# Two attention blocks on one core: a second Strassen step in layer 1's q, and the statistics of x on ScalarE

## The chip, the core and the metric

The kernel runs on one core of one Trainium2 chip. The metric is device time in microseconds, the median over three runs. The engines of the core work from queues of their own: TensorE (PE, with its weight loads shown apart as PEld), VectorE (DVE), ScalarE (ACT), GpSimd (POOL), and SyncE (SP), which issues most transfers. All data are float32. On PE a float32 matmul is two instructions in the profile, each with a weight load.

## What is computed

Two layers over eight samples of 512 channels x 1024 positions. Layer 0 is attention with eight heads after a norm over 32 groups. Layer 1, where the change lies, norms the whole sample with one mean and one variance, and has one head:

```python
def _L1_conv_ref(x, gn_gamma, gn_beta, wq, bq, wk, bk, wv, bv, wo, bo):
    mean = jnp.mean(x, axis=(1, 2, 3), keepdims=True)
    var = jnp.var(x, axis=(1, 2, 3), keepdims=True)
    n = (x - mean) * jax.lax.rsqrt(var + EPS)
    n = n * gn_gamma[None, :, None, None] + gn_beta[None, :, None, None]
    nf = n.reshape(b, c, h * w)
    q = jnp.einsum('oc,bcs->bos', wq, nf) + bq[None, :, None]
    k = jnp.einsum('oc,bcs->bos', wk, nf) + bk[None, :, None]
    v = jnp.einsum('oc,bcs->bos', wv, nf) + bv[None, :, None]
    attn = jnp.einsum('bci,bcj->bij', q, k) * c ** (-0.5)
    attn = jax.nn.softmax(attn, axis=-1)
    out = jnp.einsum('bcj,bij->bci', v, attn)
    out = jnp.einsum('oc,bcs->bos', wo, out) + bo[None, :, None]
    return x + out.reshape(b, c, h, w)
```

## The kernel before

**Folded weights.** Before the first sample the kernel multiplies layer 1's wq with wk (`wqk1`, L1728) and wv with wo (`wvo1`, L1725), so that layer 1 has one product "q" (x by wqk1, scored against x itself) and one product "v". Mean and deviation of x are taken out of the products: x goes into the matmuls as it is, and `Norm.untaken` (L350) and `Norm.bias` (L359) give small vectors that put the norm back.

**Strassen.** A product of 512 x 512 by 512 x 1024 is cut into 2 x 2 blocks and done with seven block products and not eight. The blocks are named A11 to A22 for the weights, B11 to B22 for the data; S1 to S4 are sums of A blocks, T1 to T4 differences of B blocks (`Combined.make`, L394, makes T1 to T4 of x on DVE, 128x1024 each). `strassen` (L414) runs the seven products for one row of blocks, c, in two banks of PSUM: `line` takes A11 B11, S2 T2, S3 T3 and A22 T4 one after the other in one running sum, whose values between are copied out (`copied`, ACT) or read (`done`); `single` takes A12 B21, S1 T1 and S4 B22. A product is written into a bank only when the bank's last value has been read. `together` (L607) takes turns between two such runs, c=0 and c=1, a step each.

**The second step.** Four of the seven products are plain (A12 B21, S1 T1, S4 B22, A22 T4); each can itself be cut into quarters and done with seven smaller ones. The kernel does so in layer 0's q and k and in layer 1's v: `by_two_steps` (L545) runs two pairs of such products in turns, then the three line products. It needs quarters of the data (`quarters_b`, L504: three DVE instructions, one of 128x512 and two of 128x256, for each of B21, T1, B22 and T4) and quarters of the weights (`WeightTwice`, L514: made once by DVE before the first sample, 16 sums of 128x128, stored to HBM by SP, and loaded for each use through ACT's queue, two transfers of 512 KB).

**A sample's order.** Layer 0's v, q and k, the scores and values of four head pairs, the projection (`project`, L1211, two `strassen` runs) whose `done` adds bias and the input to give x; then `attention1` (L1260): q (`make_q`, L1288, two `strassen` runs of one step), v (`make_v_twice`), scores, exponentials, values, output. The order on PE, ACT and DVE is written out by hand: each engine works in the order in which the code emits. `at_steps` (L619) runs a generator and after step n calls the functions that stand under n in a table of hooks; so DVE's other work is put between the products by number of step.

**Statistics of x.** In the projection `Norm.of_half` (L317) takes DVE's bn_stats of each 128x512 half chunk as soon as it is written, and after the stage `of_channels` (L320) aggregates four chunks. In q, `mean_of_all` (L325, after step 2) sends the chunk means through a small matmul on PE (`sample_average`, L296), reduces it on DVE and forms the spread with three DVE instructions; `deviation` (L335, after step 4) sends that through PE again, and POOL raises it to -1/2; `untaken` follows at step 5. `make_q`'s results leave by ACT with a scale per output row, the layer's gamma (L1296).

**Buffers.** PSUM has two tags, `s` and `o`, two buffers each of two banks; a `strassen` run takes one of each. SBUF tiles of 4 KB a partition come from one pool of 36 (`tile2`); weights from a pool of three (`wpool`).

## Time and profile before

| | us |
|---|---|
| median of three runs | 2830.75 (2830.41 to 2830.96) |
| the profiled execution | 2830.62 |
| its span, first to last instruction | 2828.9 |
| DVE 128x512 add out of PSUM (L1292), mean of one | 0.68 |
| DVE 128x512 bn_stats (L318), mean of one | 0.69 |
| DVE 128x1024 difference for T (L400), mean of one | 1.22 |
| ACT 128x512 copy out of PSUM (L425), mean of one | 0.58 |
| POOL 128x512 add (L1345), mean of one | 1.27 |
| POOL 128x256 add (L477), mean of one | 0.74 |
| POOL power of 128x1 (L339), mean of one | 1.46 |

The time of one is from its start to its end; on DVE and ACT the next instruction can begin some 0.1 before the end of the last. A stage is found by its lines: in the third sample the projection (L632 with `w_p`) goes from 938.70 to 963.33, layer 1's q (L632 with `w_wqk`) from 963.33 to 987.81, and v (L890) begins there.

### The profile page before, as it was taken

The page shows a single profiled execution, that of the slowest core. Times are in us where ns is not written, and L with a number is a line of the kernel's source. Part 1 is how long each engine was busy: PE and PEld are TensorE (multiplying, and loading weights), DVE is VectorE, ACT ScalarE, POOL GpSimd, SP SyncE. Part 2 cuts the span into 40 slices and gives each one's busy share as a digit, 9 for nine tenths or more (in the row PEclk, how much of TensorE's full clock was granted, in tenths as well). Part 3 has the DMA queues.
Part 4 walks back from the last instruction along what each step waited for, and adds up shares of the span by engine and source line. Part 5 has one row for each costly group of instructions (what it writes and reads, how often), then busy time and mean ns, then how long its engine had stood idle before and what let it go on. Part 6 is the DMA issues. An engine that isn't in the chain of part 4 may idle for free.

```text
span 2828.9 us, 38606 instructions
## 1 busy us (share of the span) xinstructions
PE 2815.1 (100%) x15496; PEld 1551.3 (55%) x15496; DVE 2124.3 (75%) x2979; ACT 1101.5 (39%) x1536; POOL 273.8 (10%) x236
## 2 busy tenths in 40 slices
PE   9999999999999999999999999999999999999999
PEld 5434765357643476445773456734567346673365
DVE  6677696767867778776777777777777776867867
ACT  3462324623256232552325523265232642326432
POOL 0000220003100040000400004000040000400011
PEclk9999999999999999999999999999999999999999
DMA  8422131321323213133131231313212141121001
GB/s 293 162 74 88 57 123 64 87 90 53 112 68 91 86 69 105 54 91 109 56 108 50 84 108 57 108 50 98 93 64 101 50 124 67 64 100 43 8 16 39
DMA packets 81123, 237.75 MB, mean 84 GB/s; under 512 B 21512, under 2 KB 22312, under 8 KB 74536
## 3 DMA queue, kind: packets, MB, share of 16 engines
q1 hardware_dynamic: 74456, 212.11, 23.2%
q10 hardware_dynamic: 6480, 23.10, 2.4%
q8 instruction: 124, 2.03, 0.3%
q14 instruction: 63, 0.52, 0.1%
HBM read 179.37 MB, written 31.98 MB: 75 GB/s over the span
## 4 chain that ended last, share of the span: by engine, by line
PE 92%; DVE 7%; issue 1%; ACT 0%; SPq 0%; DMA 0%; POOL 0%; DVEq 0%; ACTq 0%; POOLq 0%
PE s L941 15%; PE ps_o L960 15%; PE ps_q L632 8%; PE ps_v L647 7%; PE ps_o L1540 7%; PE ps_p L632 6%; PE ps_l_qk L869 5%; PE ps_l L1376 4%; PE ps_s L1359 4%; PE ps_s_qk L862 4%; PE ps_l_v L647 3%; PE ps_s L1376 3%; PE ps_o_qk L862 3%; PE ps_s_v L890 2%; PE ps_s_two L1670 2%; PE ps_o_v L890 1%
## 5 line engine op out<-in xcount | busy, mean ns | idle before, releaser
L798 ACT ACTIVATE p<-s 128x1024 f32<-128x1024 f32 x512 | 523.8, 1025 | 329.1 <-PE s L941 322.2
L800 DVE TENSOR_TENSOR acc<-acc,p 128x1024 f32<-128x1024 f32 x384 | 469.5, 1223 | 100.9 <-ACT p L798 92.9
L960 PE MATMUL ps_o<-p,v 64*64 64x512 f32 x4096 | 528.7, 589 | 0.0
L941 PE MATMUL s<-c_q,c_k 64*64 64x512 f32 x3584 | 465.1, 590 | 0.0
L960 PEld LDWEIGHTS ps_o<-p,v 64*64 64x64 f32 x4096 | 156.6, 133 | 282.8 <-issue 278.3
L941 PEld LDWEIGHTS s<-c_q,c_k 64*64 64x64 f32 x3584 | 134.7, 133 | 253.2 <-issue 236.1
L339 POOL TENSOR_TENSOR rstd<-rstd,minus_half 128x4 f32<-128x4 f32 (+1 forms) x16 | 19.8, 1241 | 2076.6 <-DVE rstd L338 2076.6
L1540 PE MATMUL ps_o<-t_p,s_v 128*128 128x512 f32 x384 | 168.2, 594 | 0.0
L800 DVE TENSOR_TENSOR acc<-p,p 128x1024 f32<-128x1024 f32 x64 | 78.3, 1223 | 80.0 <-ACT p L798 80.0
L1350 ACT ACTIVATE p<-p,factor 128x512 f32<-128x512 f32 (+1 forms) x112 | 85.3, 780 | 115.7 <-DVE p L1386 90.9
L1364 ACT COPY p<-ps_s 128x512 f32<-128x512 f32 x96 | 53.1, 588 | 178.7 <-PE ps_s L1359 178.7
L1540 PEld LDWEIGHTS ps_o<-t_p,s_v 128*128 128x128 f32 x384 | 72.3, 190 | 91.3 <-issue 89.2
L1386 DVE TENSOR_TENSOR p<-ps_l,p 128x512 f32<-128x512 f32 x136 | 90.1, 683 | 40.5 <-PE ps_l L1376 40.1
L632 PE MATMUL ps_q<-t,w_wqk 128*128 128x512 f32 x256 | 116.1, 598 | 0.0
L632 PE MATMUL ps_p<-t_p,w_p 128*128 128x512 f32 x256 | 112.6, 592 | 0.8 <-DVE inv L812 0.8
L425 ACT COPY u_v<-ps_v 128x512 f32<-128x512 f32 x48 | 28.1, 586 | 204.9 <-PE ps_v L647 179.6
L1386 DVE TENSOR_TENSOR p<-ps_s,p 128x512 f32<-128x512 f32 x112 | 74.8, 685 | 37.9 <-PE ps_s L1376 37.9
L647 PE MATMUL ps_v<-w_v,t_again 128*128 128x256 f32 x448 | 99.0, 379 | 0.0
L425 ACT COPY u_p<-ps_p 128x512 f32<-128x512 f32 x48 | 28.1, 586 | 169.3 <-PE ps_p L632 169.3
L425 ACT COPY u_q<-ps_q 128x512 f32<-128x512 f32 x54 | 31.3, 579 | 160.6 <-PE ps_q L632 160.6
L647 PEld LDWEIGHTS ps_v<-w_v,t_again 128*128 128x128 f32 x448 | 85.1, 190 | 11.6
L632 PE MATMUL ps_p<-o,w_p 128*128 128x512 f32 x192 | 88.6, 597 | 2.3 <-DVE o L980 2.3
(463 smaller groups left out, 4911.3 us busy)
## 6 DMA issues: line engine op xcount, KB each, us to landing
x<-in_x SPq DMA_DIRECT2D x92, 512.0 KB, 6.5
w_qk<-stored_qk SPq DMA_DIRECT2D x14, 1792.0 KB, 7.3
w_wqk<-stored_wqk SPq DMA_DIRECT2D x8, 1792.0 KB, 7.5
fold<-acc SPq DMA_DIRECT2D x56, 256.0 KB, 3.1
inv<-inv_rows SPq DMA_DIRECT2D x56, 256.0 KB, 5.0
qk_twice<-stored_qk_twice ACTq DMA_DIRECT2D x28, 512.0 KB, 6.6
w_wvo<-stored_wvo SPq DMA_DIRECT2D x8, 1792.0 KB, 7.5
out<-x SPq DMA_DIRECT2D x28, 512.0 KB, 4.6
```

The lines of the kernel that those rows point to most:

```text
L632: nc.tensor.matmul(bank, w[a][:, k, c * P : (c + 1) * P], bs[b][:, k, :], start=fresh and k == 0, stop=k == 1, skip_group_check=True,)
L647: nc.tensor.matmul(bank[:, u * 2 * P : (u + 1) * 2 * P], bs[b][:, k, n * P : (n + 1) * P], w[a][:, k, :], start=fresh and u == k == 0, sto ...
L798: nc.scalar.activation(p, s, AF.Exp, scale=factor)
L800: nc.vector.tensor_tensor(acc, first, p, ALU.add)
L862: nc.tensor.matmul(bank[:, i * 2 * P : (i + 1) * 2 * P], parts[a][x], twice_b[v][y], start=start and i == 0, stop=True, skip_group_check=True,
L869: nc.tensor.matmul(bank, of(i, a)[:, k, :], bs[v][:, k, :], start=start and k == 0, stop=k == 1, skip_group_check=True,)
L941: nc.tensor.matmul(s[cols, j, :], ks[pair][k0 // HALF][rows, k0 % HALF : k0 % HALF + HD], qs[pair][g][rows, :], start=True, stop=True,)
L960: nc.tensor.matmul(o[cols, half, :], vs[kt][rows, c0 : c0 + HD], p[rows, j, :], start=kt == 0, stop=kt == NT - 1,)
L1359: nc.tensor.matmul(bank, bs[v][:, k, t * P : (t + 1) * P], q_parts[a][:, k, :], start=a == "A11" and k == 0, stop=k == 1, skip_group_check ...
L1376: nc.tensor.matmul(bank[:, u * 2 * P : (u + 1) * 2 * P], v[y][:, u * P : (u + 1) * P], a[x], start=start and u == 0, stop=True, skip_group ...
L1386: nc.vector.tensor_tensor(at(r, t), bank, at(r, t), ALU.add)
L1540: nc.tensor.matmul(bank, v_parts[kt // 2][a][:, kt % 2, c * P : (c + 1) * P], p_parts[kt // 2][b][:, kt % 2, cols], start=fresh and kt == ...
```

## The change

q of layer 1 gets the second step. `make_q` becomes one generator of 20 steps with its own order: of the pair A12 B21 with S4 B22 two products, both line products A11 B11, the other five products, both S2 T2, the seven products of the pair S1 T1 with A22 T4, both S3 T3. One pair runs at a time, in two banks of tag `s`; the two lines take one `o` buffer each. The projection's hooks load the weights' quarters (`ready.load`) and make the quarters of B22 and B21; T1's and T4's are made in q.

The statistics of x leave DVE: `moments` has ACT go over a half chunk twice, once for the mean and once for the squares around the first half's mean, with the sums taken by the accumulator; six half chunks in the projection's `done`, the last two in q after steps 1 and 2. `both_halves` joins them with seven POOL instructions of 128x4, and the three of the spread go to POOL too. `mean_of_all` moves to step 9, `deviation` to 10, `untaken` to 14.

The scale per output row can no longer be applied on the way out, so gamma is multiplied into both sides of wqk1 before the first sample: eight DVE instructions with a row of gamma (a new input, broadcast to all partitions by one DMA) take the place of eight ACT instructions, and `WeightTwice("wqk1")` is made and stored after that of qk02.

```diff
+        def scale_both(self, by, row):
+            for cc in range(NC):
+                for to, a in self.moving(cc):
+                    nc.vector.scalar_tensor_tensor(
+                        a, a, vec[:, by + cc : by + cc + 1], row[:, to], ALU.mult, ALU.mult
+                    )
...
+        def pass_over(self, cc, half, name, func, **args):
+            to = onepool.tile([P, HALF], FP, tag="held", name=f"{name}_{self.name}_{cc}_{half}")
+            nc.scalar.activation(to, piece(self.xs, cc, half), func, **args)
+
+        def moments(self, cc, half, first):
+            mean, part = self.stat[:, 0, cc : cc + 1], self.part[:, cc, 0 if first else 1, :]
+            self.pass_over(
+                cc, half, "mean", AF.Identity, scale=1.0 / HALF,
+                accum_out=mean if first else part[:, 1:2],
+            )
+            self.pass_over(
+                cc, half, "square", AF.Square, bias=mean, scale=-1.0, accum_out=part[:, 0:1]
+            )
+
+        def both_halves(self):
+            mean, var = self.stat[:, 0, :], self.stat[:, 1, :]
+            (q0, q1), d = (self.part[:, :, i, 0] for i in range(2)), self.part[:, :, 1, 1]
+            nc.gpsimd.tensor_tensor(d, d, mean, ALU.subtract)
+            nc.gpsimd.tensor_tensor(q0, q0, q1, ALU.add)
+            nc.gpsimd.tensor_scalar(d, d, 0.5, None, ALU.mult)
+            nc.gpsimd.tensor_scalar(var, q0, 1.0 / N, None, ALU.mult)
+            nc.gpsimd.tensor_tensor(mean, mean, d, ALU.add)
+            nc.gpsimd.tensor_tensor(d, d, d, ALU.mult)
+            nc.gpsimd.tensor_tensor(var, var, d, ALU.subtract)
...
         def mean_of_all(self):
+            engine = nc.gpsimd if self.width == 1 else nc.vector
...
+    PAIRS_Q = [[("A12", "B21"), ("S4", "B22")], [("S1", "T1"), ("A22", "T4")]]
...
@@ project: done @@
-                    norm.of_half(chunk, half)
+                    if i == half or i == 1:
+                        norm.moments(chunk, half, i == half)
+                    if (i, half, c) == (1, 0, 1):
+                        ready.halve("B21")
...
+        hooks[0] = [ready.load]
+        hooks[7] = [lambda: ready.halve("B22")]
+        at_steps(together(project(w, 0), project(w, 1)), hooks)
-        for cc in range(NC):
-            norm.of_channels(cc)
...
+    class Ready:
+        def __init__(self, xs, b):
+            self.combine, self.quarters, self.b = Combined(f"1_{b}"), {}, b
+            self.combine.take(xs)
+        def load(self):
+            self.weights = WeightTwice("wqk1")
+        def halve(self, name):
+            self.quarters[name] = quarters_b(
+                self.combine.parts[name], tile2(f"{name}_twice_{self.b}")
+            )
...
+        def make_q(w):
+            parts = ready.weights.all(columns_of(w))
+            first, second = ([tile2(f"{n}_q_1_{b}_{r}") for r in range(2)] for n in ["c11", "c22"])
+            lines = [banks("o", f"ps_l{r}_q_1_{b}")[:, 0, :] for r in range(2)]
+            def pair(products, to, name):
+                line, single = (banks("s", f"ps_{name}{n}_q_1_{b}")[:, 0, :] for n in range(2))
+                def add(at, bank):
+                    nc.vector.tensor_tensor(at, bank, at, ALU.add)
+                for bank, x, y, start, use, r, t in [
+                    (line, "A11", "B11", True, nc.scalar.copy, 0, 0),
+                    (single, "A12", "B21", True, add, 0, 0),
+                    (line, "S2", "T2", False, nc.scalar.copy, 0, 1),
+                    (single, "S1", "T1", True, nc.scalar.copy, 1, 1),
+                    (line, "S3", "T3", False, add, 1, 1),
+                    (single, "S4", "B22", False, add, 0, 1),
+                    (line, "A22", "T4", False, nc.scalar.copy, 1, 0),
+                ]:
+                    for i, (a, v) in enumerate(products):
+                        nc.tensor.matmul(
+                            bank[:, i * 2 * P : (i + 1) * 2 * P], parts[a][x], twice_b[v][y],
+                            start=start and i == 0, stop=True, skip_group_check=True,
+                        )
+                    use(
+                        to[r][:, :, t * 2 * P : (t + 1) * 2 * P],
+                        bank.rearrange("p (i q) -> p i q", i=2),
+                    )
+                    yield
+            def multiply(r, a, v, fresh):
+                by_channels(w.parts[0], r, bs)(lines[r], a, v, fresh)
+            def final(r, i, half, x, y):
+                n = r + 2 * i
+                nc.vector.scalar_tensor_tensor(
+                    piece(qs, n, half), x, norm.c[:, n : n + 1], y, ALU.add, ALU.add
+                )
+            def take(r):
+                c11 = first[r][:, 0, :]
+                nc.vector.tensor_tensor(c11, lines[r], c11, ALU.add)
+            def c12_of(r):
+                c12 = first[r][:, 1, :]
+                nc.vector.tensor_tensor(c12, lines[r], c12, ALU.add)
...
+            quarters = pair(PAIRS_Q[1], second, "s")
+            for n in range(7):
+                next(quarters)
+                if n == 2:
+                    c12_of(0)
+                if n == 4:
+                    c12_of(1)
+                yield
+            for r in range(2):
+                nc.scalar.activation(
+                    piece(qs, r, 0), first[r][:, 0, :], AF.Identity, bias=norm.c[:, r : r + 1]
+                )
+                final(r, 0, 1, second[r][:, 0, :], first[r][:, 1, :])
+            for r in range(2):
+                multiply(r, "S3", "T3", False)
+                for n, half in enumerate([1, 0]):
+                    final(r, 1, half, lines[r], second[r][:, n, :])
+                yield
+
+        at_steps(make_q(w), {
+            1: [lambda: norm.moments(0, 1, False), lambda: combine.make(1)],
+            2: [lambda: norm.moments(1, 1, False)],
+            3: [lambda: combine.make(2), norm.both_halves],
+            7: [lambda: combine.make(4)],
+            8: [lambda: twice_w.append(WeightTwice("wvo1"))],
+            9: [norm.mean_of_all, lambda: ready.halve("T1")],
+            10: [norm.deviation, lambda: ready.halve("T4")],
+            12: [lambda: combine.make(3)],
+            14: [norm.untaken],
         })
...
+        gamma_row = tile2("gamma_row")[:, 0, :]
+        nc.sync.dma_start(gamma_row, gamma1.to_broadcast([P, C]))
...
-            wqk1.scale_rows(V_NW1)
+            wqk1.scale_both(V_NW1, gamma_row)
...
-            7: [wqk1.finish], 8: [waiting[0].finish], 9: [lambda: WeightTwice("qk02", both_of(w))],
+            7: [wqk1.finish], 8: [waiting[0].finish], 9: [
+                lambda: WeightTwice("qk02", both_of(w)), lambda: WeightTwice("wqk1", columns_of(wqk1)),
+            ],
```

In the part of `make_q` left out, `take(0)` stands with the third product of the first pair and `take(1)` with the seventh.

## The prediction

> **What bounds the kernel now.** I read the engines' busy times first, then the chain that ended last, then the two stages that the change touches (layer 0's projection and layer 1's q, in the third sample) as windows, and last the order of instructions on each engine there.
>
> ```profile
> PE 2815.1 (100%) x15496; PEld 1551.3 (55%) x15496; DVE 2124.3 (75%) x2979; ACT 1101.5 (39%) x1536; POOL 273.8 (10%) x236
> PE 92%; DVE 7%; issue 1%; ACT 0%; SPq 0%; DMA 0%; POOL 0%; DVEq 0%; ACTq 0%; POOLq 0%
> ```
>
> ```profile
> 938.70:963.33 24.63, 24.30 (x57) 10.55 (x56) 17.81 (x28) 3.52 (x6) 0.00 (x0) 1.00 0.21 76
> 963.33:987.81 24.48, 24.48 (x61) 11.08 (x60) 18.88 (x41) 8.61 (x13) 1.47 (x1) 1.00 0.34 118
> ```
>
> TensorE (PE) is on 92% of the chain, at full clock. The windows (length, then busy time of PE, weight loads, DVE, ACT, POOL, then clock and DMA) are the projection and q: PE is without a gap in q, and DVE is already busy for 18.9 of its 24.5 us. So whatever takes matmul time out of q shortens the run one for one, and whatever makes PE wait for DVE or ACT there lengthens it one for one.
>
> **Durations.** The rows behind every step below:
>
> ```profile
> 963.33 7.03 PE L632 MATMUL ps_q<-x,w_wqk 128*128 128x512 f32 x16
> 970.20 1.88 PE L632 MATMUL ps_q<-t,w_wqk 128*128 128x512 f32 x4
> 222.13 0.59 PE L862 MATMUL ps_s_qk<-x,w_qk 128*128 128x256 f32 x2
> 222.56 0.59 PE L862 MATMUL ps_s_qk<-t,w_qk 128*128 128x256 f32 x2
> ...
> 2638.19 0.62 ACT L808 ACTIVATE held_inv<-inv 128x512 f32<-128x512 f32 x1
> 2638.71 0.19 ACT L808 ACTIVATION_READ_ACCUMULATOR held_inv<-inv 128x1 f32 x1
> 2638.99 1.02 ACT L798 ACTIVATE p<-s 128x1024 f32<-128x1024 f32 x1
> ```
>
> Sixteen instructions of 512 columns go from 963.33 to 970.20, 0.429 us each; a float32 matmul is two of them, 0.858. Two of 256 columns are 0.432 apart (222.13 to 222.56), one matmul. A ScalarE pass over 128x512 with a sum takes 0.80 (2638.19 to 2638.99), the reading of the accumulator included. DVE and the bank hand-over are seen here:
>
> ```profile
> 957.69 0.67 DVE L1231 TENSOR_TENSOR u_p<-ps_p,u_p 128x512 f32<-128x512 f32 x1
> 958.40 0.75 DVE L1217 SCALAR_TENSOR_TENSOR x<-u_p,bias,x 128x512 f32<-128x512 f32 x1
> 959.18 0.69 DVE L318 BATCH_NORM_STATS2 part<-x 128x6 f32<-128x512 f32 x1
> 959.79 0.73 DVE L1217 SCALAR_TENSOR_TENSOR x<-ps_p,bias,x 128x512 f32<-128x512 f32 x1
> 965.25 0.59 ACT L425 COPY u_q<-ps_q 128x512 f32<-128x512 f32 x1 [8.00 <-PE ps_q L632]
> ```
>
> A DVE instruction lets the next begin 0.60 later, or about 0.75 later if it reads the result. A bank whose last matmul issues until 965.05 is read from 965.25: 0.20. PE starts some 0.05 after a release.
>
> **Part 1, the matmuls.** Before, q is 28 matmuls of 512 columns: 28 x 0.858 = 24.04 us. After, 12 of 512 (A11 B11, S2 T2, S3 T3, two rows, two each) and 28 of 256: 12 x 0.858 + 28 x 0.432 = 22.41. Saved 1.63 us a sample, 13.0 over eight. This is certain by the diff; the rest is whether PE can run them without waiting.
>
> **Part 2, the projection stage, ACT.** DVE loses eight bn_stats (0.60 each) and the aggregates, and gets the halves of B21 and B22 (each 0.6 + 0.33 + 0.33 with gaps for dependence, 1.5). ACT gets six half chunks of two passes. The first pass I take at 0.80; the Square has a bias per partition that no row of this form shows: lower end 0.71, without the accumulator's reading, upper 1.10, with a wait for the mean just read; I take 0.90, nearest to the row of 0.80. So 1.7 us for a half chunk, against an ACT queue that stands in program order. I walked the queues of the third sample with these durations (the same walk over the old order gives q from 963.23 to 987.72; the trace has 963.33 and 987.81).
> - c=0's first chunk is done at 944.4. Two passes (to 946.1) and two DMA issues of the new weights (0.45 each, by the issues of wvo_twice) stand ahead of c=1's copy, which starts at 947.0 instead of 944.65. DVE's add ends at 948.4; S1 T1 of c=1, due at 947.8, waits for that bank: 0.6 lost.
> - At S3 T3 the passes for chunk 2 (957.65 to 959.4) stand ahead of c=1's copy, ready at 957.2. DVE, which needs the copy, idles 2.5 us, and has the two halvings behind it. Chunk 1's last half is finished at 969.0; the old order has it at 966.1.
>
> **Part 3, q.** DVE's list: ten adds on banks or lines (6.0), four T's (4 x 1.13), two halvings (3.0), six final sums (6 x 0.66), small steps (some 2), plus the lag from the projection: about 22 us in a stage that PE wants to do in 22.7. A pair alternates between two banks, so each bank has 0.865 us between its products, and evacuation costs 0.20 + 0.59 + 0.05 on ACT or 0.20 + 0.69 + 0.05 on DVE: no slack. PE's waits in the walk:
> - the second product needs the bank of c=1's A22 T4, which DVE reads only at 965.2: 1.2;
> - the copy of S2 T2 stands behind the four passes over chunks 0 and 1 (968.2 to 971.7); S3 T3, in the same bank, starts 0.35 late;
> - in the second pair the adds stand behind the halves of T4, T3 and the small steps of `untaken`: 0.1 + 0.2 + 0.55, and 0.1 elsewhere.
> Sum 2.5, where the old order has 0.17. Net a sample: 0.6 + 2.5 - 0.2 - 1.6 = +1.3 us; over eight +10.7.
>
> GpSimd's ten small steps have no row. POOL takes 0.74 for 128x256 and 1.27 for 128x512, so some 0.2 for almost nothing; lower end a memset's 0.10, upper 0.75. At 0.3, which I take, the mean is there 3 us before its matmul; at 0.75 PE waits 1.4 more a sample. The Trainium skill, GPSIMD Engine Reference, § 4.1 Engine selection, says elementwise work belongs on VectorE; it speaks against this move, but at its ratio of about two (0.4 a step by DVE's 0.2) the sum stays as it is, since these steps have cover.
>
> The Trainium skill's ScalarE: Activation LUTs, § What ACT_TABLE_LOAD costs, makes the passes cheaper than the row: 186 ns + 0.833 ns an element, 93 ns for a pointer operand, 93 ns of overlap, so 0.52 and 0.61 and nothing for the accumulator. By it the walk ends at -0.1 a sample, -1 over eight; by the row's 0.80 it is +10.7.
>
> **Part 4, start and end.** Before sample 0 DVE gets eight scalings of 128x256 (0.40 each from TENSOR_TENSOR's 0.34 apart; 3.2) that were ACT's, and sixteen sums for `WeightTwice("wqk1")` (3.7, as the sixteen for qk02 took from 61.27 to 65.00). The cover is visible:
>
> ```profile
> 65.00 0.68 DVE L681 TENSOR_TENSOR v<-ps_v,u_v 128x512 f32<-128x512 f32 x1
> ...
> 66.74 2.54 PE L647 MATMUL ps_v<-w_v,t 128*128 128x256 f32 x11
> ```
>
> The add at 65.00 frees the bank that PE needs at 66.74: 1.0 of slack, and DVE's idle gaps before it are 2.1 (0.81, 0.97 and 0.34, before the sums of q, of k and of w_v). Of 6.9 added, 6.9 - 3.1 = 3.8 reaches PE; w_v's load, issued at 52.77 and now behind the later sums of wvo1, adds up to 0.8: +4.4, ends 3 and 6. The gamma row is one more DMA on SP ahead of everything that waits: nothing, 0.3 if it is not covered. The two stores on SP go ahead of the c_q loads, which have 10 us of room. In the last sample the passes of two chunks come together ahead of a copy that S3 T3 needs at 2668.9 and gets at 2670.5: +1.0 beyond the others, ends 0 and 2.
>
> **Sum.** 10.7 + 4.4 + 1.0 = 16.1 on the profiled execution's own 2830.62 us (span 2828.9 and 1.7 around it; the median, 2830.75, is 0.1 above): 2846.7, said as 2846. With the low ends (passes 0.62 + 0.71, POOL 0.10) a sample is +0.25, in all 2830.6 + 2 + 3 = 2836; with the high ends (Square 1.10, POOL 0.75) +3.8, in all 2830.6 + 30 + 8 = 2869. These two bound the forecast's own range.
>
> **Rivals.**
> 1. *The waits close and the saving shows.* If ACT's queue yields its copies in time, PE keeps its 22.7 us in q, -13.0; start-up still costs 4.4: 2822. For it: ACT is idle 21 of 24.6 us in the projection and DVE loses five us there. Against it: both queues go in program order, and DVE's list fills q. It decides if a half chunk costs under about 1.1 us of ACT and the pair's hand-over stays under 0.865.
> 2. *It evens out.* Half of the walk's waits appear: 8 x (0.6 + 2.3) / 2 - 13.0 + 4.4 = +3, 2834; within the noise.
> 3. *GpSimd becomes the bound.* If a small step costs the 1.2 that the pow takes (rows of 1.0 and 1.46), seven in line end after the mean's turn on PE, and the three between mean and deviation hold PE again: the walk gives +7.3 a sample, 2831 + 58 + 5 = 2894. Against it: the pow is no plain add, and 128x256 adds take 0.74.
>
> **Chances.** Forecast 0.62, rival 1 0.20, rival 2 0.12, rival 3 0.06. A measurement of this kernel tells 0.2% (5.7 us) from no change. Forecast and rival 3 are slower: 0.68; rival 1 faster, 0.20; rival 2 same, 0.12. The forecast's own range is 2836 to 2869. For eight in ten I reach down to 2822, where rival 1 lies, and cut the top at 2863.
>
> **What would show it.** Right: q some 25 us long in a sample with PE waiting for DVE x L1217 at its second product and for ACT copies in the first pair; DVE over 20 us busy in q; S1 T1 of c=1 in the projection waiting 0.6; the v stage of sample 0 with a wait of 4 us at its second product. Wrong: accumulating passes at 0.5, a q stage of 23 us without waits, PE's start of v in sample 0 unmoved; or a mean matmul waiting for POOL.

## The result and the profile after

| | us |
|---|---|
| before, median of four runs | 2830.69 (2830.41 to 2830.96) |
| after, median of four runs | 2844.23 (2842.13 to 2844.64) |
| ratio, 95% interval | 1.0046 (1.0034 to 1.0059) |
| the profiled execution after, and its span | 2844.26, 2842.4 |

The changed kernel is slower by 13.5 us, where 15.3 had been forecast. The page of the changed kernel, its engines' busy times and the shares of the chain that ended last:

```profile
PE 2816.7 (99%) x15688; PEld 1582.2 (56%) x15688; DVE 2136.9 (75%) x2963; ACT 1167.6 (41%) x1752; POOL 299.4 (11%) x316
...
PE 87%; DVE 9%; ACT 1%; issue 1%; DMA 1%; SPq 0%; POOL 0%; ACTq 0%; DVEq 0%; POOLq 0%
```

PE's share of the chain falls from 92% to 87% and DVE's rises from 7% to 9%: PE now waits for DVE in places. The windows of the projection and of layer 1's q in the third sample (columns as before: length, busy times of PE, weight loads, DVE, ACT, POOL, clock, DMA):

```profile
947.97:972.77 24.80, 24.30 (x57) 10.50 (x56) 14.52 (x23) 9.81 (x23) 0.00 (x0) 1.00 0.32 117
972.77:997.79 25.02, 24.29 (x86) 14.90 (x85) 22.29 (x39) 11.60 (x26) 4.74 (x11) 1.00 0.33 116
```

q is now 25.02 us long instead of 24.48, although its matmuls are shorter by 1.63; DVE is busy for 22.29 of them instead of 18.88. PE's timeline in q shows where the time goes (start, length, then engine, line and operands; in brackets the idle time before and who ended it):

```profile
972.77 1.03 PE L1360 MATMUL ps_f_q<-x,w_wqk 128*128 128x256 f32 x4
974.53 1.13 PE L1360 MATMUL ps_f_q<-x,w_wqk 128*128 128x256 f32 x4 [0.73 <-DVE x L1254]
975.49 3.60 PE L669 MATMUL ps_l_q<-x,w_wqk 128*128 128x512 f32 x8
...
985.44 1.96 PE L669 MATMUL ps_l_q<-t,w_wqk 128*128 128x512 f32 x4
987.40 0.38 PE L307 MATMUL ps_v<-spread,in_sample 128*128 128x4 f32 x2
...
989.46 3.01 PE L1360 MATMUL ps_s_q<-T_twice,wqk_twice 128*128 128x256 f32 x12
992.31 1.11 PE L1360 MATMUL ps_s_q<-t,wqk_twice 128*128 128x256 f32 x4
993.39 1.13 PE L1360 MATMUL ps_s_q<-T_twice,w_wqk 128*128 128x256 f32 x4
```

L1360 is the pair's product, L669 a row's product, L1254 the add that finishes a chunk of x, L307 the small matmul of mean and variance. A pair's product issues for 0.865 us, so the second one could have begun at 973.64; it begins at 974.53: 0.9 lost. The variance's matmul comes 0.24 late (the row's product ahead of it ends at 987.16), S4 B22 of the second pair 0.26 (992.05 to 992.31) and A22 T4 0.22 (993.17 to 993.39). With seven gaps of 0.07 to 0.15 the sum is 2.3.

The largest single loss is at the start. PE in sample 0's v of layer 0 (L684), and windows behind it:

```profile
60.67 7.07 PE L684 MATMUL ps_v<-w_v,x 128*128 128x256 f32 x32
71.73 15.24 PE L684 MATMUL ps_v<-w_v,t 128*128 128x256 f32 x56 [3.99 <-DVE v L718]
```

```profile
66.00:72.00 6.00, 2.01 (x10) 1.45 (x9) 5.83 (x25) 0.59 (x1) 0.00 (x0) 0.90 0.92 328
72.00:75.40 3.40, 3.40 (x9) 2.68 (x10) 2.66 (x5) 0.00 (x0) 0.00 (x0) 0.50 1.02 415
75.40:79.00 3.60, 3.60 (x13) 3.00 (x12) 0.00 (x0) 0.00 (x0) 0.00 (x0) 0.69 0.84 223
```

PE stands for 3.99 us behind the v add (L718), and then the 56 instructions that follow take 15.24 us where they took 12.25 before: the granted clock, third from the end of a row, is 0.50 and then 0.69. Layer 0's q begins at 91.99 instead of 84.00.

The 13.5 us of difference between the two spans, put together from the starts of layer 1's v in each sample:

| where | us |
|---|---|
| start-up, to layer 0's q of sample 0 | +8.0 |
| eight samples at +0.52 (a period of 347.52 instead of 347.00, the commonest values) | +4.2 |
| the rest of the six full periods (one is 348.67) | +1.5 |
| the last sample, beyond that (2.07 in all) | +1.5 |
| behind the last sample's v | -1.7 |

### The profile page after: what moved, and what is told of

Same layout as the page of the kernel before. It is cut to its first block, busy times and chain, and to the rows that moved or that the text cites. A ratio compares the mean times of both kernels' runs of the same rounds, so it can differ in the third digit from the quotient of the medians.

```text
span 2842.4 us, 39376 instructions
## 1 busy us (share of the span) xinstructions
PE 2816.7 (99%) x15688; PEld 1582.2 (56%) x15688; DVE 2136.9 (75%) x2963; ACT 1167.6 (41%) x1752; POOL 299.4 (11%) x316
## 4 chain that ended last, share of the span: by engine, by line
PE 87%; DVE 9%; ACT 1%; issue 1%; DMA 1%; SPq 0%; POOL 0%; ACTq 0%; DVEq 0%; POOLq 0%
PE s L978 15%; PE ps_o L997 15%; PE ps_o L1655 7%; PE ps_v L684 7%; PE ps_l_qk L906 4%; PE ps_l L1491 4%; PE ps_s L1474 4%; PE ps_s_qk L899 3%; PE ps_p L669 3%; PE ps_l_v L684 3%; PE ps_l_q L669 3%; PE ps_s L1491 3%; PE ps_o_qk L899 3%; PE ps_s_v L927 2%; PE ps_s_q L1360 2%; PE ps_s_two L1785 2%
## 5 line engine op out<-in xcount | busy, mean ns | idle before, releaser
L669 PE MATMUL ps_p<-t_p,w_p 128*128 128x512 f32 x256 | 112.9, 593 | 1.7 <-ACT u_p L461 1.0
L684 PE MATMUL ps_v<-w_v,t_again 128*128 128x256 f32 x448 | 99.0, 379 | 0.0
L669 PE MATMUL ps_p<-o,w_p 128*128 128x512 f32 x192 | 88.8, 598 | 3.4 <-DVE o L1017 3.4
L1271 DVE TENSOR_TENSOR u_p<-ps_p,u_p 128x512 f32<-128x512 f32 x48 | 33.0, 688 | 78.2 <-ACT u_p L461 77.7
L684 PEld LDWEIGHTS ps_v<-w_v,t_again 128*128 128x128 f32 x448 | 85.1, 190 | 11.6
L684 PE MATMUL ps_v<-w_v,x 128*128 128x256 f32 x384 | 86.8, 379 | 0.0
L669 PEld LDWEIGHTS ps_p<-t_p,w_p 128*128 128x128 f32 x256 | 48.4, 190 | 63.7 <-issue 53.1
```

The costliest lines, as they stand in the source:

```text
L669: nc.tensor.matmul(bank, w[a][:, k, c * P : (c + 1) * P], bs[b][:, k, :], start=fresh and k == 0, stop=k == 1, skip_group_check=True,)
L684: nc.tensor.matmul(bank[:, u * 2 * P : (u + 1) * 2 * P], bs[b][:, k, n * P : (n + 1) * P], w[a][:, k, :], start=fresh and u == k == 0, sto ...
```

## The experiments

All kernels are the changed kernel with the edit shown. "Gain" is against 2844.23; the ratio is to the kernel before, measured beside it (medians of 2829.6 to 2830.8).

| kernel | median us | ratio to before, 95% | sample's period | PE's wait at the start |
|---|---|---|---|---|
| 1, sums of wqk1 on GpSimd | 2839.18 | 1.0034 (1.0021 to 1.0046) | 347.52 | 1.47, clock 1.00 |
| 2, half of them | 2841.36 | 1.0037 (1.0023 to 1.0050) | 347.53 | 2.71, clock 0.50 |
| 3, B22's sums later | 2836.57 | 1.0021 (1.0012 to 1.0031) | 346.53 | 4.02, clock 0.50 |
| 4, small steps later | 2846.47 | 1.0058 (1.0044 to 1.0072) | 347.93 | 3.99 |
| 5, statistics on VectorE | 2852.20 | 1.0079 (1.0065 to 1.0094) | 348.83 | 4.01 |
| 6, passes over 8 columns | see there | | 346.70 | |
| 7, 3 and the wqk1 sums in v | 2830.75 | 1.0001 (0.9992 to 1.0010) | 346.55 | 0.19, clock 1.00 |
| 8, more moves | 2841.14 | 1.0040 (1.0027 to 1.0053) | 347.79 | none |
| 9, the same with another bank | 2842.95 | 1.0046 (1.0032 to 1.0060) | 348.00 | 0.24 |
| 10, the copy first | 2834.88 | 1.0020 (1.0011 to 1.0029) | 346.53 | 3.97 |
| 11, PE kept busy | 2840.48 | 1.0039 (1.0025 to 1.0052) | 347.52 | 0.49, clock 1.00 |
| 12, the best of them | 2827.62 | 0.9992 (0.9983 to 1.0001) | 346.2 to 346.4 | 0.32 |

### The start: whose sums, and the clock (1, 2 and 11)

```diff
-lambda: WeightTwice("wqk1", columns_of(wqk1)),
+lambda: WeightTwice("wqk1", columns_of(wqk1), (nc.gpsimd, nc.gpsimd)),
```

> The sixteen sums of WeightTwice("wqk1") before sample 0 go from VectorE to GpSimd; nothing else changes. Theory: the changed kernel loses 8 us before sample 0's second stage, of which 4.0 is PE's wait for the v add at 71.00 (it stands behind those sums, 4.6 us of VectorE) and 3.0 is PE at a granted clock of 0.50 to 0.69 from 72 to 79, which follows from the wait. Without the sums the add is done at about 66.4, PE never stops, the clock stays 1.00 and both are gone: 2844.2 - 7.0 = 2837, and the 56 instructions of the v stage's second half take 12.2 us as before, not 15.2. Rival 1: the low clock has another cause (the sums' or the transfers' activity): only the wait goes, 2840, and the profile still shows about 0.5 there. Rival 2: GpSimd's sums hold VectorE up or release the weights' slot too late: 2844 or more.

In kernel 2 half of the sums move:

```diff
-lambda: WeightTwice("wqk1", columns_of(wqk1)),
+lambda: WeightTwice("wqk1", columns_of(wqk1), (nc.vector, nc.gpsimd)),
```

> Only the second eight of the sixteen sums go to GpSimd, so VectorE ends 2.3 us earlier and PE's wait at the second product of sample 0's v shrinks from 4.0 to about 1.7 us. Theory: the clock falls only after a wait as long as 4 us; after 1.7 it stays at 1.00, and the kernel gains 2.3 + 3.0 = 5.3: 2839. Rival: any wait at this place lowers the clock, or the clock falls for a cause that has nothing to do with the wait: it gains 2.3, 2842, and the profile shows a clock near 0.5 behind the wait.

In kernel 11 the sums stay, and PE is given four matmuls that nobody reads, in the free half of a bank whose copy is done:

```diff
+        if b == 0:
+            def keep_busy():
+                for n in range(4):
+                    nc.tensor.matmul(idle[-2], in_sample, bs["B11"][:, 0, :], start=True, stop=True)
+            hooks[1] = [keep_busy]
```

> Four matmuls of 512 columns whose result nobody reads are added in sample 0's v stage, where PE waits 4.0 us for VectorE; the wait for the v add itself stays. Theory: the low clock (0.50 to 0.69 for 7 us, 3.0 us more for the 56 instructions that follow) comes from PE's standing idle: with 3.4 of the 4.0 us filled the clock stays at 1.00, the 56 instructions take 12.3 us instead of 15.2, and the kernel gains 1.5 to 3.0: 2841 to 2842.5. Rival: the low clock comes from something else at this time (the transfers, VectorE's load), stays in the profile, and the time is 2844.

Kernel 1 gains 5.1, kernel 2 2.9 and kernel 11 3.8. Kernel 1 stays 2 us behind its expectation: the sixteen sums are 3.7 us of DVE (67.27 to 71.00 in the changed kernel) and not 4.6, and beside GpSimd DVE's other sums are slower (see the end), so that a wait of 1.47 is left. PE at the second half of v, in kernels 1, 2 and 11 in turn (L686 and L720 are L684 and L718 there, L960 the four matmuls):

```profile
69.52 12.35 PE L686 MATMUL ps_v<-w_v,t 128*128 128x256 f32 x56 [1.47 <-DVE v L720]
```

```profile
70.81 14.04 PE L686 MATMUL ps_v<-w_v,t 128*128 128x256 f32 x56 [2.71 <-DVE v L720]
```

```profile
66.69 3.60 PE L960 MATMUL ps_v<-x,in_sample 128*128 128x512 f32 x8
70.78 12.35 PE L686 MATMUL ps_v<-w_v,t 128*128 128x256 f32 x56 [0.49 <-DVE v L720]
```

Kernel 11 decides it: from v's first instruction to its second half it is as long as in the changed kernel (59.78 to 70.78, 11.00; 60.67 to 71.73, 11.06), but PE does not stand idle, and the 56 instructions take 12.35 instead of 15.24 at a clock of 1.00. Of its 3.8 us this is 2.9; the other 0.9 is the earlier start of v, which lies between 59.78 and 61.08 in the profiles of the changed kernels. So the low clock comes from the idle time and is a cost of its own, 1.5 to 3.0 us on top of 4.0: the same 4-us wait was followed by 13.73 us in kernel 4 and 13.78 in kernel 10, by 14.94 in kernel 3 and 15.00 in kernel 5. In kernel 2 my expectation failed in both numbers: the wait was 2.71 and not 1.7 (eight sums are 1.9 us of DVE and not 2.3, and GpSimd's made DVE's slower, see the end), and the clock fell after it all the same.

### The second product of q (3 and 10)

Kernel 3 takes DVE's three sums for B22 from ahead of the projection's last adds to behind q's first product; kernel 10 leaves them and lets ACT make c=1's copy of S3 T3 ahead of the two passes over chunk 2:

```diff
-        hooks[7] = [lambda: ready.halve("B22")]
+        hooks[7] = [lambda: ready.begin("B22")]
...
+            0: [ready.end],
```

> VectorE's three sums for the quarters of B22 are issued behind the first product of q's first pair instead of ahead of the projection's last adds. Theory: PE's wait of 0.73 to 0.9 us at the second product of the first pair, once a sample, comes from VectorE's add of the last chunk to x, late by these 1.5 us of sums: without them the add starts as soon as its bank is ready (972.85 in the third sample instead of 973.73) and the wait goes: 8 x 0.87 = 7.0 us, 2837. Rival 1: B22's T2 is then finished only at the moment at which the second-level S2 T2 wants it, and VectorE's list is as long as before, so that half or all of the wait turns up there or in the second pair: 2840 to 2844. Rival 2: the wait is the hand-over of the bank and stays: 2844.

```diff
-                    if i == half or i == 1:
+                    if (i, half, c) == (1, 1, 0):
+                        due.append(lambda: norm.moments(chunk, half, True))
+                    elif i == half or i == 1:
+                        if i == half == 1:
+                            due.pop()()
                         norm.moments(chunk, half, i == half)
```

> One move alone: in the projection ScalarE's two passes over chunk 2 (row i=1, second half, c=0) are issued behind c=1's copy of S3 T3 instead of ahead of it. Theory: that copy is ready at 966.1 in the third sample by the 1.72 us rhythm of the copies before it and is made at 968.04, behind passes that themselves wait for VectorE's add; VectorE idles 2.15 us for it and is late by that much at q's second product. With the copy first, the wait of 0.87 at that product goes: 8 x 0.82 to 0.87 = 6.6 to 7, 2837.5, and the sample's period falls from 347.52 to about 346.7, as with the shortened passes. Rival: the passes over chunks 2 and 3, now one behind the other, come late for the mean or for q's first copy, and PE waits there: 2842 or more.

Either one takes the wait away, and the period falls by 0.99 to 346.53 in both; the medians gain 7.7 and 9.4 (in its profile kernel 10 has 1.5 of the second from a shorter stretch of low clock at the start). PE at q's first two products in kernel 10, now one group without a gap (in kernel 3 too, from 970.14):

```profile
969.56 1.89 PE L1364 MATMUL ps_f_q<-x,w_wqk 128*128 128x256 f32 x8
```

The mechanism is best seen on ACT, in the changed kernel:

```profile
964.39 0.59 ACT L461 COPY u_p<-ps_p 128x512 f32<-128x512 f32 x1 [1.13 <-PE ps_p L669]
966.57 0.63 ACT L335 ACTIVATE mean<-x 128x512 f32<-128x512 f32 x1 [1.59 <-DVE x L1254]
...
968.04 0.56 ACT L461 COPY u_p<-ps_p 128x512 f32<-128x512 f32 x1
```

and in kernel 10:

```profile
961.17 0.58 ACT L461 COPY u_p<-ps_p 128x512 f32<-128x512 f32 x1 [1.13 <-PE ps_p L669]
962.89 0.58 ACT L461 COPY u_p<-ps_p 128x512 f32<-128x512 f32 x1 [1.13 <-PE ps_p L669]
963.37 0.63 ACT L335 ACTIVATE mean<-x 128x512 f32<-128x512 f32 x1
```

The copies have a rhythm of 1.72. In the changed kernel the last one comes 3.65 after the one before, since it stands behind the two passes, and the first of them waits 1.59 us for DVE's add. By the rhythm the copy could have started at 966.11; ACT idles until 966.57, 0.46 longer, and the two passes then take 1.47: 1.93 late. DVE then waits for the copy:

```profile
965.74 0.75 DVE L1254 SCALAR_TENSOR_TENSOR x<-u_p,bias,x 128x512 f32<-128x512 f32 x1
968.64 0.69 DVE L1271 TENSOR_TENSOR u_p<-ps_p,u_p 128x512 f32<-128x512 f32 x1 [2.15 <-ACT u_p L461]
```

DVE idles 2.15 (0.24 in kernel 10), and the add that q's second product needs is as late. Two queues in program order wait for each other in turn, and it takes both, the late copy and B22's 1.5 us of sums, to make PE wait.

### What the statistics cost (5 and 6)

Kernel 5 keeps the second step and gives the statistics back to DVE; the passes in q and GpSimd's `both_halves` go too:

```diff
-                    if i == half or i == 1:
-                        norm.moments(chunk, half, i == half)
+                    norm.of_half(chunk, half)
...
+        for cc in range(NC):
+            norm.of_channels(cc)
```

> The second Strassen step is kept, but x's statistics go back to VectorE: a BATCH_NORM_STATS2 behind each add to x and the four aggregates at the projection's end, in place of ScalarE's sixteen passes and GpSimd's seven steps. Theory: PE waits in q for VectorE's list, not for ScalarE's; eight instructions of 0.6 and 0.4 for the aggregates lengthen that list by 5.3 us ahead of q, some 2 us of which fall into VectorE's idle time in the projection, so that the second product of the first pair is later by 2 to 3 us a sample: 2844 + 8 x 2 to 3 = 2860 to 2868. Rival: ScalarE's passes, which stand ahead of the copies, are what makes PE wait (the walk of the prediction had 0.6 in the projection and 0.35 in q for them): without them the time falls to 2844 - 8 x 0.5 to 1 = 2836 to 2840.

It is 8.0 us slower than the changed kernel. PE in its third sample, the two waits at q's second and sixth product of the first pair:

```profile
976.61 1.13 PE L1361 MATMUL ps_f_q<-x,w_wqk 128*128 128x256 f32 x4 [1.23 <-DVE x L1254]
...
985.50 1.13 PE L1361 MATMUL ps_f_q<-B_twice,w_wqk 128*128 128x256 f32 x4 [0.53 <-DVE c_q L1349]
```

The direction is the theory's, the size is half of it: the second product's wait grows by 0.5, not by 2 to 3, since without the passes ACT's copies are on time and DVE gets its 2.15 us of idle time back. Most of the rest is the wait at the first pair's last product, 0.70 where the changed kernel has 0.15; another 0.25 lies between the two line products. So with this order of products the statistics are better on ACT, by 1.3 us a sample (348.83 to 347.52).

Kernel 6 keeps the passes and makes them short:

```diff
-            nc.scalar.activation(to, piece(self.xs, cc, half), func, **args)
+            nc.scalar.activation(to[:, :8], piece(self.xs, cc, half)[:, :8], func, **args)
```

> ScalarE's sixteen passes a sample run over 8 columns of each half chunk instead of 512, so the statistics, and with them layer 1's output, are of 8 columns; the order and number of instructions stay. Theory: the passes cost little: only the copy of S3 T3 for c=1, 0.45 us late in the third sample, and the last sample's 1.0; the add that frees q's second product comes 0.45 earlier, 8 x 0.45 + 1 = 4.6, 2839.6. Rival 1 (the prediction's walk): the passes hold PE up by 0.6 in the projection and 0.35 in q besides: some 8 x 1.4 + 1 = 12, 2832. Rival 2: they lie wholly beside other work: 2844.

Its time, 8022 us, answers another question: with statistics of 8 columns the values leave the bound that the kernel tests at its end (`sums_good`, `all_good`), and a second, general pass runs behind the first. In its profile the first pass can still be read: a period of 346.70, 0.82 less, and 327.32 in the last sample instead of 329.93. So the passes cost, in this order, about 7 x 0.82 + 2.6 = 8.4 us, between the two expectations, and the place is the one of kernel 10: the copy comes 2.81 behind the one before it, not 3.65. The 0.83 by which the two passes ahead of it are shorter (0.64 instead of 1.47) is as much as the period loses; with the copy ahead of them, in kernel 10, passes of full length give a period that is shorter still, 346.53.

### What is moved takes its bank with it (4, 8 and 9)

Kernel 4 moves the variance's matmul one product later and `untaken` two:

```diff
-            10: [norm.deviation, lambda: ready.halve("T4")],
-            14: [norm.untaken],
+            10: [lambda: ready.halve("T4")],
+            11: [norm.deviation],
+            16: [norm.untaken],
```

> Two moves of small steps in q: the variance's matmul one product later (behind the first product of the second pair), and the four small VectorE steps of untaken behind the sixth product of the second pair instead of behind the fourth. Theory: PE waits 0.24 us a sample at the variance's matmul for GpSimd's three steps between mean and deviation, and 0.2 at the second pair's A22 T4 for the add behind untaken; both go: 8 x 0.44 = 3.5 us, 2840.7. Rival: VectorE's list in q is full, and what is taken from one product is paid at the next: 2844, with the waits moved to other rows.

```profile
987.57 0.28 PE L307 MATMUL ps_v<-spread,in_sample 128*128 128x4 f32 x2
988.41 1.13 PE L1360 MATMUL ps_s_q<-t,w_wqk 128*128 128x256 f32 x4 [0.56 <-DVE mean_v L309]
```

It is 2.2 slower: the variance's matmul takes a buffer of the tag `s` out of turn, and the second pair's next product waits 0.56 for DVE to read it. By the period it loses more, 8 x 0.41 = 3.3; its profile has a shorter stretch of low clock at the start, worth 1.5. Kernel 8 has kernel 7's moves (below), takes the free half of row 0's bank for the two small matmuls, and puts row 0's S3 T3 between S3 T3 and S4 B22 of the second pair; in its last sample two groups of passes come later. Kernel 9 is kernel 8 with row 1's bank (`reversed(lines)` in the first line) and with ACT's passes moved as in kernel 10; its last sample has one of the two groups still later. Of kernel 8's edit:

```diff
+            spares[:] = [t[:, 1, :] for t in lines]
...
+                if n == 4:
+                    multiply(0, "S3", "T3", False)
+                    yield
...
-            8: [lambda: twice_w.append(WeightTwice("wvo1"))],
-            9: [norm.mean_of_all, lambda: ready.halve("T1")],
+            8: [norm.mean_of_all, lambda: twice_w.append(WeightTwice("wvo1"))],
+            9: [lambda: ready.halve("T1")],
...
-            14: [norm.untaken],
+            17: [norm.untaken],
```

> The same, and besides: the mean's and variance's matmuls take the unused halves of the banks of the rows' products instead of banks of the pairs, and the mean's comes one product earlier; row 0's S3 T3 runs between the second pair's S3 T3 and S4 B22, with untaken behind S4 B22; in the last sample the passes over the first two chunks stand behind the copies of S2 T2. Theory: the variance's wait (0.24 a sample), most of the hand-over waits at S4 B22 and A22 T4 (0.26 and 0.22) and the last sample's 1.0 go: 8 x 0.24 + 8 x 0.3 + 1 = 5.3 less than the same without them, 2825. Rival: VectorE's list is full and each move is paid at the next product: 2830 to 2831, no gain.

> As the kernel with all moves, with three things changed: the mean's and variance's matmuls take the free half of row 1's bank instead of row 0's (row 0's next product waited 1.35 us a sample for VectorE's reading of the mean); the passes over chunk 2 in the projection stand behind c=1's copy of S3 T3 instead of ahead of it; in the last sample the first chunk's passes stand behind the copies of S2 T2 and the second's behind the projection's last product. Theory: q then has only the second pair's hand-over left and takes 23.4 us instead of 24.0, of which 0.2 comes back as a wait for a bank in v; the last sample loses its wait of 1.0: 8 x 0.4 + 1 = 4 less than the kernel with the two moves alone (2830.75), 2827, 0.1% less than the kernel before. Rival: VectorE is the bound once PE stops waiting, and what q gives v takes back: 2830.

Both fail at the mean. PE in kernel 8 and in kernel 9:

```profile
977.36 3.70 PE L669 MATMUL ps_l_q<-t,w_wqk 128*128 128x512 f32 x8 [1.35 <-DVE mean_m L309]
```

```profile
977.62 0.35 PE L307 MATMUL ps_l_q<-stat,in_sample 128*128 128x4 f32 x2 [1.49 <-DVE c_q L1400]
```

In the one the row's product waits until DVE has read the mean from the other half of its buffer, in the other the mean's matmul waits until DVE has read the row's; waits are kept per buffer of two banks, so the halves aren't free of each other. Without that wait kernel 8's period would be 347.79 - 1.35 = 346.44, where kernel 7 has 346.55: what the second pair gains, v takes back with a wait for row 1's bank. That the second pair's hand-over waits are worth little alone is so far an inference; kernel 12, below, bears on it.

### Two moves together, and the best version (7 and 12)

Kernel 7 is kernel 3 with the sixteen sums emitted inside sample 0's v:

```diff
+        if b == 0:
+            hooks[3] = [lambda: WeightTwice("wqk1", columns_of(wqk1))]
```

> B22's sums behind the first product of q, and the sixteen sums of WeightTwice("wqk1") not ahead of sample 0's v stage but inside it, behind its fourth product, where VectorE is idle. Theory: the start-up wait of 4.0 and the low clock behind it (1.5 to 3.0 by the profiles so far) go, without the slowing of VectorE that GpSimd's sums brought; the v add is done at 67.9 at the latest and PE waits 0.4 or less: -5 to -6.5 beside the -7.7 of B22's sums, 2830 to 2831.5, level with the kernel before. Rival: the two overlap or the sums in the v stage delay its own adds: 2834 to 2836.

It comes out as expected, level with the kernel before. Kernel 12 has these sums, kernel 10's copy, row 0's S3 T3 between the second pair's products, T3 made right behind T2, and the last sums in an order that frees row 1's bank for v:

```diff
+                if n == 4:
+                    multiply(0, "S3", "T3", False)
+                    yield
...
-                final(r, 0, 1, second[r][:, 0, :], first[r][:, 1, :])
             for r in range(2):
-                multiply(r, "S3", "T3", False)
+                if r:
+                    multiply(r, "S3", "T3", False)
                 for n, half in enumerate([1, 0]):
                     final(r, 1, half, lines[r], second[r][:, n, :])
-                yield
+                final(r, 0, 1, second[r][:, 0, :], first[r][:, 1, :])
+            yield
...
-            3: [lambda: combine.make(2), norm.both_halves],
+            3: [lambda: combine.make(2), norm.both_halves, lambda: combine.make(3)],
...
-            12: [lambda: combine.make(3)],
-            14: [norm.untaken],
+            17: [norm.untaken],
```

> Two moves that have each shown their gain (the passes over chunk 2 behind c=1's copy; the sums of WeightTwice("wqk1") in sample 0's v stage), and one that tries for more: row 0's S3 T3 between the second pair's S3 T3 and S4 B22, with T3 made right behind T2 where VectorE idles 1.03 us, untaken behind S4 B22, and the last sums in an order that frees row 1's bank first for v. Theory: the two moves give 2844.2 - 8 x 0.85 - 6.5 = 2831, level with the kernel before; the third removes the hand-over waits of 0.26 and 0.22 a sample without the wait for a bank in v: 8 x 0.4 = 3, 2828, and a sample's period of 346.1 instead of 346.53. Rival: v takes back what q gains, period 346.5, 2831.

```profile
982.51 1.88 PE L669 MATMUL ps_l_q<-t,w_wqk 128*128 128x512 f32 x4
984.23 1.03 PE L1366 MATMUL ps_s_q<-t,wqk_twice 128*128 128x256 f32 x4
985.10 1.03 PE L1366 MATMUL ps_s_q<-T_twice,w_wqk 128*128 128x256 f32 x4
985.96 1.88 PE L669 MATMUL ps_l_q<-t,w_wqk 128*128 128x512 f32 x4
987.67 0.61 PE L927 MATMUL ps_s_v<-w_wvo,x 128*128 128x128 f32 x4
```

S4 B22 and A22 T4 now run without a gap behind row 0's product, and v begins with no wait for a bank. q takes 23.70 us, a sample 346.2 to 346.4, where the theory had 346.1 and the rival 346.5: against kernel 10's 346.53 the third move, which does away with the hand-over waits of 0.26 and 0.22, was worth 0.1 to 0.3 a sample. At 2827.62 it is 16.6 us faster than the changed kernel; against the kernel before, 0.9992 (0.9983 to 1.0001), it can't be told from equal, the less so as its profile lacks the low clock that the kernel before has in the last sample, 1.7 us (see the end). Of the 1.63 us that the shorter matmuls save, 0.6 to 0.8 a sample remain.

## Why the prediction was right, and where it was not

The sign was right, and the mechanism in two of three places: PE waits in q for DVE's late list, and at the start for the v add behind the new sums. That the time came so near (2844.23 for 2846) is in part luck: the eight samples were forecast at +10.7 and cost +5.7, the start at +4.4 and cost +8.0, the last sample at +1.0 and +1.5, and -1.7 at the end has nothing to do with the change.

1. *The matmuls, -1.63 a sample.* Borne out by the sum: 22.41 of matmuls, 0.28 for the two small ones and the 2.3 of waits read above make 25.0; q was 25.02.
2. *ACT in the projection, first place.* "S1 T1 of c=1 ... waits for that bank: 0.6 lost." This step failed, and with it 4.8 of the forecast's us. The two passes cost what was said, 1.67 for 1.70 (954.01 to 955.68). (The lower price that the prediction sets beside the row, 0.52 and 0.61, does not hold here: the passes take 0.75 and 0.92 to the next instruction, with 0.19 in each for the accumulator.) But I let the two DMA issues stand in line behind them at 0.45 each; in the trace they lie beside the square pass, and the copy follows the passes at once:

```profile
954.76 0.72 ACT L335 ACTIVATE square<-x,stat 128x512 f32<-128x512 f32 x1
954.83 0.33 ACTq L560 DMA_DIRECT2D wqk_twice<-stored_wqk_twice  x1
955.25 0.39 ACTq L561 DMA_DIRECT2D wqk_twice<-stored_wqk_twice  x1
955.39 0.19 ACT L335 ACTIVATION_READ_ACCUMULATOR square<-x,stat 128x1 f32 x1
955.68 0.59 ACT L461 COPY u_p<-ps_p 128x512 f32<-128x512 f32 x1
```

PE does not wait at S1 T1 of c=1. The projection's only wait in this sample is 0.50 for DVE's `o`; it is 0.33 in most others, as in the kernel before.
3. *ACT in the projection, second place.* "The passes for chunk 2 ... stand ahead of c=1's copy ... DVE idles 2.5": 2.15. Kernel 10 shows that this one inversion, with B22's sums behind it, is the whole of the second product's wait. I had taken it as given by the queues; the order was free to change.
4. *The waits in q, 2.5 a sample.* 2.3 in sum. The second product took 0.9 for 1.2; S3 T3 of the first pair hardly waits (0.35 had been said); the second pair's places are right, 0.08, 0.26 and 0.22 for 0.1, 0.2 and 0.55. What was missing is the variance's matmul, 0.24 late behind GpSimd's three steps (985.88 to 987.35). I costed GpSimd's steps only ahead of the mean, where the cover was there (3.8 us), and behind it only in rival 3. A tensor_tensor took 0.20 to 0.39, near the 0.3 that I took, but the first tensor_scalar of each group 1.21 and 0.66.
5. *The sum per sample, +1.3.* 0.52 by the periods: too high by the 0.6 of point 2 and by 0.2 of point 4.
6. *The start, +4.4.* 8.0. The wait was 3.99 for 3.8. What the step lacked is the clock behind it, 3.0 us, shown by kernel 11; and v itself starts 0.85 later: PE is 0.28 behind when the first product of layer 0's q begins (33.98 for 33.70) and loses the rest between the products of that q and k, which I had not counted; why is open. w_v's load, which I had counted, shows on DVE: it waits 1.12 for it instead of 0.34, and that lies within the 3.99.
7. *The last sample, +1.0.* It loses 1.5 beyond the others; a wait of 0.99 for the copy behind four passes is where it was said to be, the other half was not followed up.
8. *Rivals.* Neither 1 (2822) nor 3 (2894) came. For the eight samples alone the outcome, +4.2 to +5.7, lies between the forecast's +10.7 and the -1.4 in rival 2; the start made up for it. What rival 1 rests on, copies that ACT yields in time, was a matter of order and not of its condition: a half chunk costs 1.67 of ACT and not under 1.1, and kernels 10 and 12 have the copies in time all the same.

Still open: one period in most of these profiles, the fifth here, is 0.4 to 1.2 us longer than its neighbours (348.67 to 347.52); in the kernel before and in kernels 5 and 11 none is. In the changed kernel it lies in the projection: PE waits 0.68 and 0.54 for DVE's `o` (L1017) where the others have one wait of 0.33 or 0.50, and DVE waits 1.06 for the transfer of `inv` (1991.65), in the other samples not. Why the transfer comes late in that one sample is open; no run was spent on it.

## What to carry to other kernels

When an engine's queue is in program order, ask of every instruction that is put into it what it waits for and who waits for what stands behind it: the same two passes, 1.5 us with a wait of 1.6 for DVE ahead of them, cost PE a microsecond a sample ahead of a copy that DVE needed, and nothing behind it. Saved matmul time is kept only as far as the engines around can follow; here reordering alone, with the same instructions, was worth 16.6 us. And a wait of PE is to be priced with the clock that follows it.

## What the runs showed of the hardware

**The clock after a pause.** PE's granted clock fell to 0.5 after waits of 3.97 to 4.02 us in each of the five profiles read for it, and after 2.71 in one. Kernel 9 waits 1.49 in every sample; in seven the clock stays at 1.00, in the last it is 0.50 from 2700.7 to 2704.1, and eight matmul instructions take 5.38 instead of 3.68. After 1.47 or less it fell nowhere. The same end of the last sample, where every kernel waits 1.95 to 1.98 us for DVE, shows both; before and after:

```profile
2721.81 8.86 PE L647 MATMUL ps_l_v<-w_wvo,t 128*128 128x256 f32 x32 [1.95 <-DVE c_v L583]
```

```profile
2737.05 7.17 PE L684 MATMUL ps_l_v<-w_wvo,t 128*128 128x256 f32 x32 [1.95 <-DVE c_v L620]
```

In the kernel before the clock is 0.58 on the mean of the 3.4 us behind it, and the 32 instructions take 1.69 more. It is so in 5 of 13 profiles (before and kernels 3, 7, 8, 9; kernel 6 is not counted), one of each kernel; this is the -1.7 in the table of differences, and no merit of the change. Read in narrow windows, the clock is 0.50 for a stretch of 3.4 us (kernels 2, 4 and 10 at the start; all of these at the end) or of 6.8 (the changed kernel, 3 and 5 at the start). It begins from 1.6 before the end of the pause to 0.8 behind it, and the price is half of what PE works in it: in the changed kernel it goes from 70.8 to 77.6, PE works from 71.73, (77.6 - 71.73) / 2 = 2.9; in kernel 4 from 71.5 to 74.9, PE from 72.07, 1.4. Measured against the 12.35 at full clock: 2.9 and 1.4. The Trainium skill, TensorE: Matmul & The Clock Gate, Part 1: The HAM clock gate, says that the array falls to half its clock after an idle window of about 3.4 us, in windows that run free of the kernel. The half rate, the length of the stretches and the chance are as it says; its rule of "no PE-idle gaps >~3.4µs" is too lax here: pauses of 2.71, 1.95 and, once in eight, 1.49 us were enough.

**GpSimd beside DVE.** In kernel 1 the sums of two SBUF operands slow each other. DVE and GpSimd, with a sum that overlaps and one that doesn't:

```profile
62.26 0.94 DVE L195 TENSOR_TENSOR w_v<-w_v,rest_v 128x512 f32<-128x512 f32 x1
```

```profile
62.61 0.90 POOL L513 TENSOR_TENSOR wqk_twice<-w_wqk 128x128 f32<-128x128 f32 x1
...
64.34 0.45 POOL L513 TENSOR_TENSOR wqk_twice<-wqk_twice,w_wqk 128x128 f32<-128x128 f32 x1
```

The same DVE sum took 0.69 in the changed kernel. So work moved to GpSimd took back part of DVE's gain, and emitting the sums where DVE is idle (kernel 7, a wait of 0.19) did more than giving them to another engine (kernel 1, 1.47). The Trainium skill's GPSIMD Engine Reference, 8. Key points, names this contention for DVE instructions with two SBUF inputs; the rows agree.
